# W2 by language in order of first appearance, W1 by id for twenty batches

## The chip, the core and the metric

The kernel runs on one core of a Trainium2 chip. The time is that of the device, in microseconds, as the median of timed runs; the profile is of one execution, taken apart from them. Engines are named as in the profile: PE (TensorE, with PEld for its weight loads), DVE (VectorE), ACT (ScalarE), POOL (GpSimd) and SP (SyncE, which here only issues DMAs).

## The reference

There are 128 batches of 128 rows by 512 columns in float32. Every batch has a language id, and ten languages have their own W1 (512 x 128), b1, W2 (128 x 512), b2, gamma and beta.

```python
def _L0_cond_ref(hidden_states, language_ids, W1, b1, W2, b2, gamma, beta):
    w1 = W1[language_ids]
    w2 = W2[language_ids]
    h = jnp.einsum('bsh,bha->bsa', hidden_states, w1) + b1[language_ids][:, None, :]
    h = jax.nn.relu(h)
    adapted = jnp.einsum('bsa,bah->bsh', h, w2) + b2[language_ids][:, None, :]
    x = hidden_states + adapted
    mean = jnp.mean(x, axis=-1, keepdims=True)
    var = jnp.mean(jnp.square(x - mean), axis=-1, keepdims=True)
    normed = (x - mean) * jax.lax.rsqrt(var + LN_EPS)
    return normed * gamma[language_ids][:, None, :] + beta[language_ids][:, None, :]
x = x + _L0_cond_ref(x, itok_B_0_8, L0_cond_W1, ...)
```

The ids are drawn from 0 to 8, so language 9 doesn't occur in this input, but the kernel doesn't know that. The kernel folds the outer sum in: the output is the normed row times gamma, plus (x + beta).

## The kernel before

A batch is one tile of 128 x 512. The main loop is a software pipeline with one turn per batch: in turn `i` it transposes x of batch `i` on PE, multiplies batch `i - 1` by its W1 (`down`), batch `i - 2` by its W2 (`up`), and does the residual, the statistics and the output of batch `b = i - 3` and of older ones. A helper, `keep`, pins every instruction behind the one recorded before it on its engine, so the order in the code is the order on each engine. SP issues nearly all the loads and the stores, in that same order; it takes them in turn on eight semaphores, so that a load is issued only when the load eight places before it has landed.

Per batch, PE makes four transposes of x into PSUM (`transpose_x`), four matmuls with W1 (`down`) and one with W2 (`up`); in fp32 these are issued as 4, 8 and 2 pieces. ACT copies the transposed x to SBUF (`copy_xT`), applies relu with b1 (`relu`), copies the batch's W1 out of the table of all ten languages (`stage_w1`), and squares (`square`); for every pair of batches it computes the mean and the inverse root (`scalar_means`, `deviation`). DVE adds the residual with a running sum (`residual`), subtracts the mean and multiplies by gamma (`scale`), and multiplies by the inverse deviation and adds what POOL prepared (`finish`). POOL adds beta to x (`add_beta`), and for most batches b2 to x (`add_b2`); where it doesn't, DVE adds b2 (`vector_b2`) or PE puts it into PSUM with a one-hot matmul (`pick`, inside `up`).

Tables that depend on the language are read at an offset held in a register: `lid(b, engine)` loads four ids at a time from `lang`. Since the offset isn't known when the program is built, an instruction that reads a table in this way waits for every write to the table that stands before it in the code. The transposed x has one PSUM buffer (`p_x`, bufs=1), so `transpose_x` of the next batch waits for `copy_xT` of this one.

Before the loop can run, three things are made ready.

- The rows of beta, gamma and b2 (ten each) are spread over all 128 partitions. They are split into three bf16 parts that add up to the fp32 value; a one-hot matmul on PE (`spread`, L202 to L211) picks a row into PSUM, and DVE or ACT copies it into `beta_b`, `gamma_b`, `b2_b`: 30 rows.
- W2 is loaded whole, in two loads (`load_w2`, 768 and 1792 KB).
- W1 for the first nine batches (`FIRST`) is loaded by id, 256 KB each, into a ring of five buffers; batches up to 20 (`EARLY` = 21) are copied by ACT from `w1e`, all ten W1 in a layout that loads quickly (two loads of 1280 KB); batches from 21 on are copied from `w1`, loaded in four chunks of 640 KB in the turns 8, 10, 12 and 14 (`load_w1`, L103).

PE first runs ten idle matmuls (`spin`) on a constant.

```python
if i in (8, 10, 12, 14):
    load_w1((i - 8) // 2)
...
if i + 1 >= LATE and on(i + 1):
    stage_w1(i + 1)
```

Of the kernel before, what the change touches and what calls it, by code (L numbers as in the profile page):

```python
# [16 lines left out]
P = 128  # L17
G = 4
EPS = 1e-5
FIRST = 9  # L20
EARLY = 21
LATE = 12
# [4 lines left out]
def cond_resid_kernel(ctx: ExitStack, tc: tile.TileContext, x, itok, W1, b1, W2, b2, gamma, beta, out):  # L27
# [31 lines left out]
    wp = ctx.enter_context(tc.tile_pool(name="wp", bufs=5))  # L59
# [18 lines left out]
    ids = const.tile([1, B], I32, name="ids")  # L78
# [3 lines left out]
    w1e = const.tile([P, L, KC, A], FP, name="w1e")  # L82
    w2 = const.tile([P, L * H], FP, name="w2")
    x_0 = xp.tile([P, G, H], FP, tag="x", name="x_0")
    xs[0] = x_0
# [5 lines left out]
    keep(nc.sync.dma_start(out=ids, in_=itok.rearrange("(o b) -> o b", o=1)))  # L91
    keep(nc.scalar.dma_start(out=rows[0:L, :], in_=beta))
    keep(nc.sync.dma_start(out=rows[L : 2 * L, :], in_=gamma))
    keep(nc.scalar.dma_start(out=rows[2 * L : 3 * L, :], in_=b2))
    load_part(0, 2)
    keep(nc.scalar.dma_start(out=b1r, in_=b1))

    warm = const.tile([P, 1], FP, name="warm")
    keep(nc.vector.memset(warm, 1.0))
    keep(nc.scalar.activation(warm, warm, AF.Abs_reciprocal_sqrt))  # L100
    def load_w1(k):
        keep(
            nc.sync.dma_start(out=w1[:, :, k, :], in_=W1[:, k * P : (k + 1) * P, :].rearrange("l p a -> p l a"))  # L103
        )

    ident = const.tile([P, P], FP, name="ident")
    make_identity(nc, ident)
    eps = const.tile([P, 1], FP, name="eps")
    nc.gpsimd.memset(eps, EPS)
    ones = const.tile([P, P], BF, name="ones")  # L110
    nc.gpsimd.memset(ones, 1.0)
# [3 lines left out]
    R = 3 * L  # L115
# [6 lines left out]
    keep(nc.vector.tensor_scalar(pick[:, L : 2 * L], pick[:, L : 2 * L], -0.5, None, ALU.mult))  # L122
# [4 lines left out]
    wrap = const.tile([1, B], I32, name="wrap")  # L127
    keep(nc.vector.tensor_scalar(wrap, ids, 0, L, ALU.is_lt, ALU.mult))
    lang = const.tile([1, B], I32, name="lang")
    keep(nc.vector.tensor_tensor(lang, ids, wrap, ALU.add))  # L130
    keep(nc.vector.tensor_scalar(lang, lang, 0, L - 1, ALU.max, ALU.min))

    def lid(b, engine):
        g = b // G
        if (g, engine) not in lids:
            loads, vals = nc.values_load_multi_w_load_instructions(  # L136
                lang[0:1, g * G : (g + 1) * G],
                engines=[engine],
                min_val=0,
                max_val=L - 1,  # L140
                skip_runtime_bounds_check_because="clamped on the chip to 0..L-1 above",
            )
            for ins in loads:
                keep(ins)
            lids[g, engine] = vals
        return lids[g, engine][b % G]

# [3 lines left out]
    def load_first(b):  # L151
        w1s[b] = wp.tile([P, KC, A], FP, tag="w1s", name=f"w1s_{b}")
        src = W1[bass.ds(lid(b, ET.SP), 1)].rearrange("o (p k) a -> p (o k a)", k=KC)
        keep(nc.sync.dma_start(out=w1s[b].rearrange("p k a -> p (k a)"), in_=src))

    def load_w2(lo, hi):
        dst = w2[:, lo * H : hi * H].rearrange("p (l h) -> p l h", l=hi - lo)
        keep(nc.sync.dma_start(out=dst, in_=W2[lo:hi].rearrange("l a h -> a l h")))

    def load_early(lo, hi):  # L160
        dst = w1e[:, lo:hi].rearrange("p l k a -> p l (k a)")
        keep(nc.sync.dma_start(out=dst, in_=W1[lo:hi].rearrange("l (p k) a -> p l (k a)", k=KC)))

    load_w2(0, 3)
    load_first(0)
    load_first(1)
    load_part(2, G)
    load_first(2)
    load_first(3)
    load_w2(3, L)  # L170
    xs[1] = xp.tile([P, G, H], FP, tag="x", name="x_1")
    for b in (G, G + 2):
        load_part(b, b + 2)
        load_first(b)
        load_first(b + 1)
    xs[2] = xp.tile([P, G, H], FP, tag="x", name="x_2")
    load_part(2 * G, 2 * G + 2)
    load_early(0, 5)
    load_first(2 * G)
    load_early(5, L)  # L180
    load_part(2 * G + 2, 3 * G)

    left = rp.tile([P, H], FP, tag="r", name="left")
    keep(nc.vector.tensor_copy(parts[0:R, :], rows[0:R, :]))
    keep(nc.vector.tensor_tensor(left[32 : 32 + R, :], rows[0:R, :], parts[0:R, :], ALU.subtract))
    keep(nc.vector.tensor_copy(parts[32 : 32 + R, :], left[32 : 32 + R, :]))
    keep(nc.vector.tensor_tensor(left[64 : 64 + R, :], left[32 : 32 + R, :], parts[32 : 32 + R, :], ALU.subtract))
    keep(nc.vector.tensor_copy(parts[64 : 64 + R, :], left[64 : 64 + R, :]))
# [7 lines left out]


    beta_b = const.tile([P, L * H], FP, name="beta_b")
    gamma_b = const.tile([P, L * H], FP, name="gamma_b")
    b2_b = const.tile([P, L * H], FP, name="b2_b")  # L200

    def spread(r, copier):  # L202
        t = (beta_b, gamma_b, b2_b)[r // L]
        row = p_y.tile([P, H], FP, tag="y", name=f"row_{r}")
        pick_r = pick[:, r : r + 1].to_broadcast([96, P])
        keep(nc.tensor.matmul(row, lhsT=pick_r, rhs=parts[:96, :], start=True, stop=True))
        dst = t[:, r % L * H : (r % L + 1) * H]
        if copier is nc.scalar:
            keep(nc.scalar.copy(dst, row))
        else:  # L210
            keep(nc.vector.tensor_copy(dst, row))  # L211
# [5 lines left out]
    def b2_by_matmul(b):  # L217
        return b in (5, B - 1)

    def b2_by_vector(b):  # L220
        return b < 4 or 8 <= b < B - 8 and (b % 4 == 1 if b < 24 else b % 16 in (1, 6, 11) or b % 32 == 30)

    def stage_w1(b):
        w1s[b] = wp.tile([P, KC, A], FP, tag="w1s", name=f"w1s_{b}")
        src = (w1e if b < EARLY else w1).rearrange("p l k a -> p (l k a)")[:, bass.ds(lid(b, ET.Activation) * (KC * A), KC * A)]
        keep(nc.scalar.copy(w1s[b].rearrange("p k a -> p (k a)"), src))  # L226

    def transpose_x(b):
        pxs[b] = p_x.tile([P, KC, P], FP, tag="xT", name=f"pxT_{b}")
        for k in range(KC):  # L230
            if b < EARLY:
                cols = xb(b).rearrange("s (p k) -> s k p", k=KC)[:, k, :]
            else:
                cols = xb(b)[:, k * P : (k + 1) * P]
            keep(nc.tensor.transpose(pxs[b][:, k, :], cols, ident))  # L235
# [32 lines left out]
    def up(b):  # L268
        v = lid(b, ET.PE)
        ys[b] = p_y.tile([P, H], FP, tag="y", name=f"py_{b}")  # L270
        m = b2_by_matmul(b)
        if m:
            pick_b = pick[:, bass.ds(v + 2 * L, 1)].to_broadcast([96, P])
            keep(nc.tensor.matmul(ys[b], lhsT=pick_b, rhs=parts[:96, :], start=True, stop=False))
        keep(nc.tensor.matmul(ys[b], lhsT=hT[b], rhs=w2[:, bass.ds(v * H, H)], start=not m, stop=True))  # L275
        del hT[b]
# [61 lines left out]
    def of_pair(g):  # L338
        if g not in parts_of:
            parts_of[g] = p_s.tile([P, 2], FP, tag="s", name=f"root_{g}"), st.tile([P, 2], FP, tag="part", name=f"part_{g}")  # L340
        return parts_of[g]
# [138 lines left out]
    def spin(n, width):  # L480
        idle = p_s.tile([P, H], FP, tag="s", name="idle")
# [8 lines left out]
    spin(9, H)  # L490
    spin(1, H // 2)

    def spread_turn(lo, hi):
        for r in range(lo, hi):
            spread(r, nc.scalar if r % 7 in (1, 3, 5) else nc.vector)
# [4 lines left out]

    x_turn(0)
    transpose_b1()
    spread_turn(0, 4)
    x_turn(1)
    spread_turn(4, 11)
    down(0)
    relu(0)
    spread_turn(11, 15)
    down(1)
    relu(1)  # L510
    x_turn(2)
    spread_turn(15, 19)
    x_turn(3)
    down(2)
    relu(2)
    spread_turn(19, 24)
    down(3)
    relu(3)
    spread_turn(24, R)
    up(0)  # L520
    up(1)

    for i in range(3, B + U):
# [3 lines left out]
        if i == 5:  # L527
            load_x(3)
        if i in (8, 10, 12, 14):
            load_w1((i - 8) // 2)  # L530
        if i == 4:
            up(2)
        if i == 5:
            up(3)
        if i > 3 and on(i):
            transpose_x(i)
        if b <= E:
            add_b2(b + 2)
            add_beta(b)
        if i > 4 and on(i - 1):  # L540
            down(i - 1)
        if i > 3 and on(i):
            copy_xT(i)
# [3 lines left out]
        if i > 4 and on(i - 1):  # L547
            relu(i - 1)
        if i + 1 >= LATE and on(i + 1):
            stage_w1(i + 1)  # L550
        if i > 5 and on(i - U):
# [41 lines left out]
        if FIRST <= i + 1 < LATE:  # L593
            stage_w1(i + 1)

        for n, engine in ((i + 3, ET.Activation), (i - U + 3, ET.PE), (b + 1, ET.DVE), (b + 5, ET.Pool)):
            if on(n):
                lid(n, engine)

# [36 lines left out]
```

## Time and profile before

| What | Value |
|---|---|
| Median of three runs | 308.69 us (307.93 to 308.85) |
| Span of the profiled execution | 306.5 us |
| Busy: PE, DVE, ACT, POOL | 294.6, 295.9, 282.3, 283.9 us |
| Moved by DMA | 77.85 MB, mean 254 GB/s |
| First transposes, first residual | 5.4 us, 20.9 us |

The profiled execution is known by its span; the timed runs include 2.2 us more around it. A line of the profile gives engine, line of the source, operation, the tiles by name (output on the left of the arrow, inputs on the right) and shapes. In a timeline the two numbers in front are the start and the duration in microseconds, and a bracket at the end says how long the engine was idle before and what ended that. In a table of stretches each row has the stretch, its length, the busy time of PE, PEld, DVE, ACT and POOL with the number of instructions, then the granted PE clock as a share of full speed, the DMA engines' busy share, and GB/s. `q` behind an engine's name is its sequencer, which issues DMAs and register loads. Names of DRAM tensors end in `_dram`; digits are left out of names, so `w` stands for `w1` as well as `w2`, and `b_b` for `b2_b`.

### The profile page before, as it was taken

Reading aid. Unit: us, or ns where it says so; the run is one execution under the profiler, and the core shown is the slowest. Engines: PE = TensorE matmul, PEld = TensorE weight load, DVE = VectorE, ACT = ScalarE, POOL = GpSimd, SP = SyncE. Lnnn points to the kernel's source line nnn. Section 1 sums busy time; section 2 is a strip of 40 time slices with the busy share of each in tenths; the row PEclk is TensorE's granted clock in tenths of the full one; section 3 lists DMA queues with packets and bytes.
Section 4 is the critical chain, followed back from the end, with each engine's and each line's share of the span. In section 5 each row is a group of like instructions: output and inputs, shape, how many; then the busy total and the mean of one; then the engine's idle time right before and its main releaser. Section 6 shows DMA issues by size and latency. Waiting matters only on the chain. (4 is left out here: it accounts for less than half of the span.)

```text
span 306.5 us, 6981 instructions
## 1 busy us (share of the span) xinstructions
PE 294.6 (96%) x1835; PEld 220.0 (72%) x1835; DVE 295.9 (97%) x771; ACT 282.3 (92%) x777; POOL 283.9 (93%) x238
## 2 busy tenths in 40 slices
PE   8999999999999999999999999999999999999960
PEld 3748787777777777777777777777777777777730
DVE  6889999999999999999999999999999999999985
ACT  3858999999999999999999999999999999999981
POOL 1349899999999999999999999999999999999994
PEclk9999999999999999999999999999999999999995
DMA  6999999976678766766777666767776666773324
GB/s 231 379 390 388 373 371 354 387 231 240 221 255 276 250 202 241 226 257 219 259 276 243 213 209 238 265 224 260 275 238 206 226 231 242 246 266 137 135 109 171
DMA packets 43769, 77.85 MB, mean 254 GB/s; under 512 B 1961, under 2 KB 7348, under 8 KB 43730
## 3 DMA queue, kind: packets, MB, share of 16 engines
q1 hardware_dynamic: 43382, 76.84, 72.1%
q10 hardware_dynamic: 348, 0.57, 0.5%
q8 instruction: 15, 0.25, 0.3%
q14 instruction: 24, 0.20, 0.2%
HBM read 43.85 MB, written 33.55 MB: 253 GB/s over the span
## 5 line engine op out<-in xcount | busy, mean ns | idle before, releaser
L252 POOL TENSOR_TENSOR o<-x,beta_b 128x512 f32<-128x512 f32 x128 | 173.9, 1395 | 10.2 <-DVE beta_b L211 9.5
L245 POOL TENSOR_TENSOR r<-x,b_b 128x512 f32<-128x512 f32 x97 | 135.7, 1399 | 7.3 <-DVE b_b L211 6.2
L258 PE MATMUL ph<-xT,w1s 128*128 128x128 f32 x1024 | 135.4, 275 | 0.0
L275 PE MATMUL py<-w,hT 128*128 x256 | 131.2, 595 | 0.5 <-DVE b_b L211 0.5
L258 PEld LDWEIGHTS ph<-xT,w1s 128*128 128x128 f32 x1024 | 124.9, 192 | 1.0 <-ACT hT L266 0.5
L235 PEld LDWEIGHTS pxT<-ident,x 128*128 128x128 f32 x512 | 66.6, 151 | 65.3 <-issue 49.2
L358 DVE SCALAR_TENSOR_TENSOR py<-py,nmean,gamma_b 128x512 f32<-128x512 f32 x126 | 95.0, 754 | 0.9 <-ACT sq L399 0.8
L367 DVE SCALAR_TENSOR_TENSOR o<-py,rstd,o 128x512 f32<-128x512 f32 x122 | 91.2, 748 | 0.0
L315 ACT ACTIVATE sq<-py,sum 128x512 f32<-128x512 f32 x124 | 85.9, 693 | 2.8 <-DVE py L292 2.5
L235 PE MATMUL pxT<-ident,x 128*128 128x128 f32 x512 | 78.2, 276 | 0.0
L239 ACT COPY xT<-pxT 128x512 f32<-128x512 f32 x128 | 74.7, 584 | 3.5 <-PE pxT L235 3.5
L292 DVE SCALAR_TENSOR_TENSOR py<-py,r 128x512 f32<-128x512 f32 x97 | 67.0, 691 | 0.2
L226 ACT COPY w1s<-w 128x512 f32 x107 | 65.5, 612 | 0.0
L266 ACT ACTIVATE hT<-ph,b1T 128x128 f32<-128x128 f32 x128 | 46.9, 366 | 7.9 <-PE ph L258 2.6
L275 PEld LDWEIGHTS py<-w,hT 128*128 128x128 f32 x256 | 39.1, 192 | 2.9 <-issue 1.0
L315 ACT ACTIVATION_READ_ACCUMULATOR sq<-py,sum 128x1 f32 x124 | 25.0, 202 | 0.0
L292 DVE SCALAR_TENSOR_TENSOR py<-py,x 128x512 f32<-128x512 f32 x31 | 21.7, 699 | 0.4
L285 DVE TENSOR_TENSOR py<-py,b_b 128x512 f32<-128x512 f32 x29 | 20.2, 695 | 0.7 <-PE py L275 0.6
L325 ACT ACTIVATE root<-ssq,eps 128x2 f32<-128x2 f32 x62 | 16.4, 265 | 0.0
L292 DVE DVE_READ_ACCUMULATOR py<-py,r 128x1 f32 x97 | 13.7, 141 | 0.0
L306 ACT ACTIVATE nmean<-sum 128x2 f32<-128x2 f32 x62 | 12.3, 198 | 0.0
L329 DVE SCALAR_TENSOR_TENSOR part<-ssq,root 128x2 f32<-128x2 f32 x62 | 9.3, 151 | 0.2 <-ACT root L325 0.2
(55 smaller groups left out, 90.4 us busy)
## 6 DMA issues: line engine op xcount, KB each, us to landing
out_dram<-o SPq DMA_DIRECT2D x61, 512.0 KB, 3.4
x<-in_x_dram SPq DMA_DIRECT2D x29, 1024.0 KB, 6.2
x<-in_x_dram SPq DMA_DIRECT2D x6, 512.0 KB, 8.8
w1e<-in_L_cond_W_dram SPq DMA_DIRECT2D x2, 1280.0 KB, 12.3
w<-in_L_cond_W_dram SPq DMA_DIRECT2D x4, 640.0 KB, 8.1
w1s<-in_L_cond_W_dram SPq DMA_DIRECT2D x9, 256.0 KB, 8.4
w<-in_L_cond_W_dram SPq DMA_DIRECT2D x1, 1792.0 KB, 10.3
w<-in_L_cond_W_dram SPq DMA_DIRECT2D x1, 768.0 KB, 5.4
```

The costliest lines, as they stand in the source:

```text
L226: keep(nc.scalar.copy(w1s[b].rearrange("p k a -> p (k a)"), src))
L235: keep(nc.tensor.transpose(pxs[b][:, k, :], cols, ident))
L239: keep(nc.scalar.copy(xT[b], pxs.pop(b)))
L245: keep(nc.gpsimd.tensor_tensor(rs[b], xb(b), b2_b[:, bass.ds(v * H, H)], ALU.add))
L252: keep(nc.gpsimd.tensor_tensor(os[g][:, j, :], xb(b), beta_b[:, bass.ds(v * H, H)], ALU.add))
L258: nc.tensor.matmul(phs[b], lhsT=w1s[b][:, k, :], rhs=xT[b][:, k, :], start=(k == 0), stop=(k == KC - 1))
L266: keep(nc.scalar.activation(hT[b], phs.pop(b), AF.Relu, bias=b1T[:, bass.ds(lid(b, ET.Activation), 1)]))
L275: keep(nc.tensor.matmul(ys[b], lhsT=hT[b], rhs=w2[:, bass.ds(v * H, H)], start=not m, stop=True))
L292: nc.vector.scalar_tensor_tensor(ys[b], ys[b], 1.0, r, ALU.mult, ALU.add, accum_out=col(sums, b))
L315: nc.scalar.activation(sq, ys[b], AF.Square, bias=col(sums, b), scale=-float(H), accum_out=col(ssqs, b))
L358: nc.vector.scalar_tensor_tensor(ys[b], ys[b], col(nmeans, b), gamma_b[:, bass.ds(v * H, H)], ALU.add, ALU.mult)
L367: nc.vector.scalar_tensor_tensor(o, ys.pop(b), rstds[g][:, j : j + 1], o, ALU.mult, ALU.add)
```

## The change

**W1.** The first 20 batches (`BY_ID`) take W1 by id, 256 KB each, into a ring that now has seven buffers; `w1e` and its two loads are gone. From batch 20 on, ACT copies W1 from `w1` as before. The loads for batch `n` are issued by `ahead(n)`, five turns ahead in the loop; `ahead` also loads x in pairs, W2, and at `n` = 9, 12, 15 and 18 the four chunks of `w1`. In the loop, `load_w1` is called with the same chunk numbers again in the turns 16, 21, 26 and 31, where it was called in the turns 8 to 14 before.

**W2.** It is no longer loaded whole. The kernel ranks the languages by first appearance among the ids: every language, on its own partition, takes the largest weight (a falling function of the position) among the batches that have it; a matmul puts these on one row for comparison, a count of larger ones is its rank, and two small matmuls turn ranks into `slots`, a list that has the language of each slot and the slot of each batch. SP loads W2 for slot after slot (ten loads of 256 KB, `load_slot`), and `up` reads it at the batch's slot. Since batch `b` has a slot of at most `b`, `up(b)` of the first ten batches waits only for the slots up to `b`.

**Rows.** Beta's ten rows are loaded four times, once for every 32 partitions, and spread by DVE with `stream_shuffle` from SBUF to SBUF. Gamma's and b2's rows still go through one-hot matmuls; gamma's are copied by ACT ahead of the loop, b2's by DVE and ACT in turn during turns 3 to 7. The first eight batches (`BY_PE`) get b2 by the matmul inside `up`, where it was DVE for batches 0 to 3, POOL for 4, 6 and 7, and the matmul for 5. The bf16 parts are made by reading the upper halves of the fp32 words.

**Order.** POOL adds beta two batches earlier than before. In a turn, `copy_xT` stands before `down`. The idle matmuls are seven instead of ten.

```diff
-FIRST = 9
-EARLY = 21
-LATE = 12
+BY_ID = 20
+BY_PE = 8
+RING = 7
...
+    keep(nc.sync.dma_start(out=lang[:, 0:B], in_=itok.rearrange("(o b) -> o b", o=1).to_broadcast([L, B])))
+    keep(nc.scalar.dma_start(out=rows[0:L, :], in_=gamma))
+    load_part(0, 1)
+    keep(nc.scalar.dma_start(out=rows[L : 2 * L, :], in_=b2))
+    for q in range(4):
+        engine = nc.sync if q % 2 else nc.scalar
+        keep(engine.dma_start(out=beta_rows[32 * q : 32 * q + L, :], in_=beta))
+    keep(nc.scalar.dma_start(out=b1r, in_=b1))
+    load_part(1, 2)
...
+    keep(nc.vector.scalar_tensor_tensor(seen, lang, own, weight, ALU.is_equal, ALU.mult))
+    keep(nc.vector.tensor_reduce(first, seen, mybir.AxisListType.X, ALU.max))
...
+    def rank_languages():
+        order = p_s.tile([P, H], FP, tag="s", name="order")
+        keep(nc.tensor.matmul(order[:L, 0:L], lhsT=first.to_broadcast([L, L]), rhs=ident[:L, :L], start=True, stop=True))
...
+        keep(nc.vector.tensor_scalar(above, order[:L, 0:L], first, None, ALU.is_gt, ALU.add, accum_out=rank))
+        keep(nc.vector.tensor_scalar(own_of, lang[:, 0:B], own, None, ALU.is_equal))
+        keep(nc.vector.tensor_scalar(place, count[:, 0:L], rank, None, ALU.is_equal))
...
+    def place_languages(order):
+        keep(nc.tensor.matmul(order[:1, L : 2 * L], lhsT=own, rhs=place, start=True, stop=True))
+        keep(nc.tensor.matmul(order[:1, 2 * L : 2 * L + B], lhsT=rank, rhs=own_of, start=True, stop=True))
+        keep(nc.vector.tensor_copy(slots, order[:1, L : 2 * L + B]))
...
+    def load_slot(j):
+        if j == 0:
+            v = lid(0, ET.SP)
+        else:
+            if not perm:
+                perm.extend(values(slots[0:1, 1:L], ET.SP, L - 1))
+            v = perm[j - 1]
+        src = W2[bass.ds(v, 1)].rearrange("o a h -> a (o h)")
+        keep(nc.sync.dma_start(out=w2[:, j * H : (j + 1) * H], in_=src))
...
+    def spread_beta(lo, hi):
+        for r in range(lo, hi):
+            keep(nc.vector.stream_shuffle(beta_b[:, r * H : (r + 1) * H], beta_rows, [r] * 32))
...
-        return b in (5, B - 1)
+        return b < BY_PE or b == B - 1
...
-        src = (w1e if b < EARLY else w1).rearrange("p l k a -> p (l k a)")[:, bass.ds(lid(b, ET.Activation) * (KC * A), KC * A)]
+        src = w1.rearrange("p l k a -> p (l k a)")[:, bass.ds(lid(b, ET.Activation) * (KC * A), KC * A)]
...
+    def ahead(n):
+        if n in (4, 6, 8, 10):
+            load_part(n, n + 2)
+        load_by_id(n)
+        if n < L + 2:
+            load_slot(n - 2)
+        if n >= 9 and n % 3 == 0:
+            load_w1((n - 9) // 3)
...
-        if i in (8, 10, 12, 14):
-            load_w1((i - 8) // 2)
...
+        if i in (16, 21, 26, 31):
+            load_w1((i - 16) // 5)
+        b2_rows = [r for r in (2 * i - 6, 2 * i - 5) if 0 <= r < L]
...
+        if i + RING - 2 < BY_ID:
+            ahead(i + RING - 2)
...
-        if i + 1 >= LATE and on(i + 1):
+        if BY_ID <= i + 1 and on(i + 1):
             stage_w1(i + 1)
```

## The prediction

> **What bounds the kernel now.** I read the page's busy times first, then stretches of ten microseconds (busy time by engine, granted clock, DMA share, GB/s), then the instructions of two turns of the loop in order of time, then the DMA issues, the waits, and last the clock at the end of the run.
>
> ```profile
> PE 294.6 (96%) x1835; PEld 220.0 (72%) x1835; DVE 295.9 (97%) x771; ACT 282.3 (92%) x777; POOL 283.9 (93%) x238
> 0.00:10.00 10.00, 8.76 (x35) 4.39 (x36) 7.25 (x19) 4.85 (x9) 0.87 (x8) 1.00 0.74 270
> 10.00:20.00 10.00, 9.54 (x60) 6.57 (x59) 7.77 (x13) 7.04 (x15) 2.83 (x3) 1.00 1.02 381
> 20.00:30.00 10.00, 10.00 (x58) 7.26 (x57) 9.63 (x23) 7.41 (x21) 10.00 (x9) 1.00 1.05 388
> 30.00:40.00 10.00, 10.00 (x65) 7.91 (x65) 9.87 (x29) 9.36 (x26) 8.86 (x8) 1.00 1.07 376
> 40.00:50.00 10.00, 10.00 (x64) 7.84 (x63) 10.00 (x25) 9.72 (x27) 9.89 (x9) 1.00 1.07 354
> 50.00:60.00 10.00, 10.00 (x66) 7.82 (x66) 10.00 (x27) 9.71 (x30) 9.46 (x9) 1.00 1.06 386
> 60.00:70.00 10.00, 10.00 (x66) 7.60 (x65) 10.00 (x28) 9.83 (x28) 10.00 (x9) 1.00 0.77 264
> ```
>
> From 20 us on four engines are full at once, so a wait on any of them is not won back later. The DMA engines are full too, but only until 60 us. Summing the GB/s column, 2.7, 6.5, 10.4, 14.2, 17.7 and 21.6 MB have moved by 10, 20, ... 60 us, 377 GB/s from 10 us on.
>
> ```profile
> 55.65 0.62 ACT L226 COPY w1s<-w1e 128x512 f32 x1
> 56.01 0.63 PE L235 MATMUL pxT<-ident,x 128*128 128x128 f32 x4
> 56.16 0.70 ACT L315 ACTIVATE sq<-py,sum 128x512 f32<-128x512 f32 x1
> 56.83 0.59 ACT L239 COPY xT<-pxT 128x512 f32<-128x512 f32 x1
> 57.57 0.37 ACT L266 ACTIVATE hT<-ph,b1T 128x128 f32<-128x128 f32 x1
> 57.83 0.61 ACT L226 COPY w1s<-w 128x512 f32 x1
> 58.23 0.60 PE L235 MATMUL pxT<-ident,x 128*128 128x128 f32 x4
> 59.16 0.27 ACT L325 ACTIVATE root<-ssq,eps 128x2 f32<-128x2 f32 x1
> 59.56 0.76 DVE L358 SCALAR_TENSOR_TENSOR py<-py,nmean,gamma_b 128x512 f32<-128x512 f32 x1
> 60.09 0.61 ACT L226 COPY w1s<-w 128x512 f32 x1
> ```
>
> The turn is 2.2 us. The copies at L226 are those of W1 for batches 20, 21 and 22. Behind each stand, on ACT, the square of an older batch, the copy of the next transposed x and the relu. VectorE's scale starts 0.1 us after ACT's root, and PE's next transposes start 0.8 us after the copy of xT began: an ACT wait reaches both almost whole.
>
> ```profile
> x<-in_x_dram SPq DMA_DIRECT2D x29, 1024.0 KB, 6.2
> w<-in_L_cond_W_dram SPq DMA_DIRECT2D x4, 640.0 KB, 8.1
> 297.00:300.00 3.00, 0.00 (x0) 0.00 (x0) 2.19 (x11) 2.28 (x7) 2.92 (x3) 1.00 0.06 21
> 300.00:302.00 2.00, 0.00 (x0) 0.00 (x0) 1.96 (x7) 0.37 (x1) 1.92 (x3) 0.50 0.34 131
> 1.19 4.45 PE L484 MATMUL idle<-ones 128*128 128x512 bf16 x10 [1.19 <-POOL ones L111]
> ```
>
> A load takes microseconds to land. PE's last matmul ends at 296.3 and 3.7 us later its clock is halved; the opening matmuls took 0.43 us each, the same 512 columns later 0.22.
>
> **The sum's base.** The profiled execution spans 306.5 us; the median of the three timed runs, 308.69, is 2.2 above. I add the parts to 306.5 and carry the 2.2.
>
> **Head, up to batch 10: -3.0, which the next part swallows.** PE's path: first x lands near 3.5 (512 KB took 3.6 from issue, 256 KB stores 2.0), W1 of batch 0 near 6.2, then two downs (0.89 each), seven gamma rows (0.22), one up with its pick (1.08): batch 3's transposes start near 11.1. Three gamma rows follow (0.66), five turns of 2.84 (transposes 0.43, two b2 rows 0.44, down 0.89, pick 0.22, up 0.86) and two of 2.40: batch 10 at 30.8, where it was 33.8. VectorE: ten shuffles have no row; the row copies of L211 took 3.82 for 6, so 0.64, and GpSimd's pass over the same tile, 1.24, is the far bound (nothing moves 512 columns in under the 0.58 of ACT's copy). I take 0.64, the same engine and tile: 6 to 12.4 us (18.5 at the far bound), before the first residual is due at about 13 (20.9 today). VectorE also loses 12 row copies against ten shuffles and four b2 adds (0.67 each); GpSimd loses three adds (1.24 each) and starts near 13 instead of 11, ACT loses eleven copies of W1 (0.51 each) and does 15 row copies instead of 13, and two of the splits. The ranking adds some eight small VectorE instructions (0.15 to 0.28 each, as at L122 to L131) and three small matmuls; the slots are there near 6.3, and SP, which needs them for its second W2 load with every later load behind it, gets there near 7. The 8 loads already issued (5.6 us of moving) cover it if it is late. The four beta loads (20 KB, two of them on SP ahead of x 1) cost SP 0.7, which is in the lag below. I cost all of it at nothing: the wait for the loads hides it, up to some 8 us; without that cover the head is worth the 3.0.
>
> **DMA order: +8.0 at batch 22.** All loads stand in SP's one queue, each behind the one eight places before. In units of 256 KB, what must have landed for batch 20's copy of w1 is x to 23 (24), W1 by id (20), W2 (10), four chunks of w1 (10), five stores (10) and the first chunk again (2.5): 76.5 units, 20.1 MB. The chunks are loaded twice: `ahead` issues them at batches 9, 12, 15, 18, and the loop again at i = 16, 21, 26, 31; the second loads are 2.6 MB more. The copies read w1 at a register's offset, so each waits for all chunks issued before it, and each reload after the first waits for the copy before. On today's curve 20.1 MB is reached at 56.4. Add 0.7, because only 0.5 MB instead of 1.3 is issued before the ids are known (bounds 0 and 1.5), and 1.4 from moving to landing (x of batches 24 to 27 is issued at 49.7, lands 8.4 later, and ends 20.3 MB in order, which the curve reaches at 56.8): 58.5. ACT stands there from 52.7 (55.65 - 3.0). It copies batch 21's W1 at about 60.5, and that releases the second reload, which is queued behind x 24 to 31 and two stores: 91 units, 23.9 MB with small ones, on the curve at 66.4, landed at 68.5. Batch 22's copy then starts at 68.5 instead of 60.1: +8.4, less 0.3 that VectorE and PE have in hand. SP's issues (0.36 to 0.47 each) are shorter than the 0.70 that 256 KB take to move, so the queue does not run dry.
>
> **The other two reloads: +3.6 and +2.2.** The queue is empty by then (share 0.77 and less). For batch 27: the copy of batch 26 ends at 69.4 on today's clock, but SP first waits for the store of batches 18 and 19 (finished at 69.8, issue 0.4). 640 KB land after 4.1 (3.6 for 512 KB in the quiet head; bounds 3.6, and 5.7, the fastest 1 MB load) plus 0.5 for that store: 74.9 against a copy due at 71.0, less 0.3. For batch 32 no store stands between: 80.3 + 0.1 + 4.1 = 84.5 against 82.0, less 0.3.
>
> **Clock: +1.3.** PE runs out of work for about 5.7 us before batch 23's transposes, longer than the 3.7 us after which the clock fell. The opening spin shows half speed for at most the first 5.3 us of work (2.6 us lost); below it is 0. I take the middle. The first wait's share is hidden by the second, the last two are shorter than 3.7. [...]
>
> Sum: 306.5 + 8.0 + 3.6 + 2.2 + 1.3 = 321.6, with 2.2 around it 323.8. After batch 32 the turn is 2.19 as before, and the tail is the same code.
>
> **Rivals.** (1) The DMA keeps ahead: batch 20's copy finds everything landed, and only three round trips are paid: -3.0, then 4.2 - 1.7 (the turn less one copy) - 0.3 = 2.2, 3.6, 2.2: 313.7. For it: waits for a landing were 1.1 and 0.5 us today. Against: a share over 1.0 up to 60 us, and more bytes. 10%. (2) Faster: the second loads hold nobody up, because nobody waits for them; then the head's gain counts, less 1.5 for W1 of batch 19 (72 units, 55.3, due 53.5): about 307. It decides at the landing: a reload that took under 1.7 us would do the same, and the shortest landing in the trace is 2.0. The copies' waits on the reloads stand in the built program. 8%. (3) Loads of 256 KB move more slowly: at three quarters of 377 GB/s the 34 of them among the 91 units (8.9 MB) take 7.9 us longer: 331.7. Against: from 10 to 20 us, with loads of 256 and 512 KB, the rate was 381, as good as any. 6%. [...]
>
> **Numbers.** Forecast 74%: its own range is 318 to 332 (a rate of 390 or 354 GB/s after 10 us puts batch 22 at 66.6 or 72.2; the bounds of landing give 1.8 to 5.2 and 1.7 to 3.8 at the reloads; 0 to 2.6 for the clock). 2% is left for what I don't see. The range, 312 to 330, adds the first rival, leaves the second and third out, and cuts the corner where every bound is at its worst. Measured runs differ by 0.3%, so faster means under 307.8: 9%, same 2%, slower 89%.
>
> **What would show it.** The ACT copies of w1 for batches 20, 22, 27 and 32 wait for a DMA, by about 6, 6, 4 and 2.5 us, and no other does; the DMA share stays over 1.0 to about 66 us; PE's clock dips once near 69 us; four more 640 KB loads are listed. Wrong would be: no waits at these copies, or batch 22's at 61 (first rival); rows of beta later than 19 us; a slower turn after batch 32.

## The result, and the profile after

The changed kernel takes 330.3 us (median, 329.2 to 331.8) beside 308.6 for the kernel before on the same chip: a ratio of 1.071, with a 95% interval from 1.068 to 1.074. It is slower, as forecast, but by 21.7 us instead of 15.1, and 0.3 us beyond the upper end of the range. The profiled execution spans 328.8 us, 22.3 more than before.

Busy times, and of the picture in 40 slices the rows for the PE clock and for the DMA, of the changed kernel:

```profile
PE 301.3 (92%) x1835; PEld 223.3 (68%) x1835; DVE 296.9 (90%) x780; ACT 280.3 (85%) x770; POOL 281.2 (86%) x239
...
PEclk9899999988989899999999999999999999999995
DMA  5999999955478267777765757686667777762344
```

Every engine has about as much to do as before, and the span is longer: the time went into waits. A slice is 8.2 us; the clock is reduced in the second and around 72, 90 and 107 us. The stretches of ten microseconds show where the waits lie (columns as before: PE, PEld, DVE, ACT, POOL busy, clock, DMA share, GB/s):

```profile
10.00:20.00 10.00, 9.81 (x56) 6.80 (x55) 5.72 (x15) 8.86 (x21) 6.85 (x6) 0.96 1.01 351
...
30.00:40.00 10.00, 9.08 (x54) 6.34 (x53) 10.00 (x22) 6.62 (x20) 5.96 (x5) 1.00 1.07 394
...
50.00:60.00 10.00, 9.54 (x59) 7.08 (x59) 9.83 (x28) 7.33 (x21) 8.01 (x7) 1.00 1.09 379
60.00:70.00 10.00, 7.15 (x44) 4.97 (x42) 8.11 (x21) 4.42 (x13) 10.00 (x9) 1.00 0.99 338
70.00:80.00 10.00, 7.18 (x41) 6.13 (x42) 4.83 (x13) 8.10 (x23) 6.57 (x6) 0.83 0.37 115
80.00:90.00 10.00, 6.09 (x36) 4.22 (x35) 5.67 (x18) 5.53 (x16) 8.62 (x7) 0.97 0.56 181
...
100.00:110.00 10.00, 6.83 (x36) 4.86 (x34) 6.50 (x18) 5.86 (x16) 7.57 (x7) 0.83 0.72 244
```

In the last four rows PE is busy for 6 to 7 us of ten, VectorE and ACT are not full either, and the DMA share falls to 0.37: everything waits for single loads. The instructions of ACT in order of time name them; the copies at L285 are those of W1 for batches 20, 21, 22, 27 and 32:

```profile
60.02 0.61 ACT L285 COPY w1s<-w 128x512 f32 x1
62.21 0.61 ACT L285 COPY w1s<-w 128x512 f32 x1
71.00 0.62 ACT L285 COPY w1s<-w 128x512 f32 x1 [6.42 <-DMA w<-in_L_cond_W_dram]
87.11 0.62 ACT L285 COPY w1s<-w 128x512 f32 x1 [4.39 <-DMA w<-in_L_cond_W_dram]
103.44 0.62 ACT L285 COPY w1s<-w 128x512 f32 x1 [3.91 <-DMA w<-in_L_cond_W_dram]
```

The loads that they wait for stand in SP's order of time, and in the list of DMA issues there are eight of 640 KB where there were four:

```profile
51.85 0.53 SPq L114 DMA_DIRECT2D w<-in_L_cond_W_dram  x1
62.84 0.70 SPq L114 DMA_DIRECT2D w<-in_L_cond_W_dram  x1
81.96 0.42 SPq L114 DMA_DIRECT2D w<-in_L_cond_W_dram  x1
97.79 0.38 SPq L114 DMA_DIRECT2D w<-in_L_cond_W_dram  x1
...
w<-in_L_cond_W_dram SPq DMA_DIRECT2D x8, 640.0 KB, 7.7
```

The second, third and fourth reload (the second loads of the chunks) let the copy start 8.2, 5.1 and 5.6 us after their issue. Batch 20's copy waits for no load: the first reload, issued at 51.85, had landed 7.7 us later, at 59.6, and ACT reached the copy at 60.0. How much later PE begins the transposes of a batch than in the kernel before tells what each of these costs:

| Batch | 10 | 20 | 22 | 23 | 24 | 27 | 29 | 32 | 35 | 127 |
|---|---|---|---|---|---|---|---|---|---|---|
| Later by, us | 3.2 | 4.4 | 4.4 | 10.2 | 11.6 | 11.6 | 17.4 | 17.4 | 22.5 | 22.5 |

So there are two parts: 4.4 us up to batch 20 (called the head below; the forecast had a gain of 3.0 by batch 10), and 7.2, 5.8 and 5.1 us at the three reloads.

### The profile page after: what moved, and what is told of

It is laid out like the page before. It is cut to its first block, busy times and chain, and to the rows that moved or that the text cites. A ratio compares the mean times of both kernels' runs of the same rounds, so it can differ in the third digit from the quotient of the medians.

```text
span 328.8 us, 7103 instructions
## 1 busy us (share of the span) xinstructions
PE 301.3 (92%) x1835; PEld 223.3 (68%) x1835; DVE 296.9 (90%) x780; ACT 280.3 (85%) x770; POOL 281.2 (86%) x239
## 5 line engine op out<-in xcount | busy, mean ns | idle before, releaser
L311 POOL TENSOR_TENSOR o<-x,beta_b 128x512 f32<-128x512 f32 x128 | 163.7, 1294 | 29.8 <-DMA out_dram<-o 13.8
L317 PE MATMUL ph<-xT,w1s 128*128 128x128 f32 x1024 | 138.4, 279 | 0.8 <-DMA w1s<-in_L_cond_W_dram 0.8
L334 PE MATMUL py<-w,hT 128*128 (+1 forms) x256 | 132.9, 601 | 0.0
L304 POOL TENSOR_TENSOR r<-x,b_b 128x512 f32<-128x512 f32 x94 | 121.8, 1297 | 12.4 <-DMA w<-in_L_cond_W_dram 7.4
L317 PEld LDWEIGHTS ph<-xT,w1s 128*128 128x128 f32 x1024 | 128.0, 196 | 1.8 <-issue 1.1
L294 PE MATMUL pxT<-ident,x 128*128 128x128 f32 x512 | 79.6, 279 | 13.3 <-ACT xT L298 12.7
L285 ACT COPY w1s<-w 128x512 f32 x108 | 66.2, 613 | 14.7 <-DMA w<-in_L_cond_W_dram 14.7
L351 DVE SCALAR_TENSOR_TENSOR py<-py,r 128x512 f32<-128x512 f32 x94 | 64.8, 689 | 2.9 <-PE py L334 2.6
L351 DVE SCALAR_TENSOR_TENSOR py<-py,x 128x512 f32<-128x512 f32 x34 | 23.7, 697 | 0.3
L344 DVE TENSOR_TENSOR py<-py,b_b 128x512 f32<-128x512 f32 x25 | 17.3, 690 | 0.9 <-PE py L334 0.8
L351 DVE DVE_READ_ACCUMULATOR py<-py,r 128x1 f32 x94 | 13.1, 139 | 0.0
L388 DVE SCALAR_TENSOR_TENSOR part<-ssq,root 128x2 f32<-128x2 f32 x62 | 10.9, 175 | 0.2 <-ACT root L384 0.2
```

The source lines that it names most:

```text
L304: keep(nc.gpsimd.tensor_tensor(rs[b], xb(b), b2_b[:, bass.ds(v * H, H)], ALU.add))
L311: keep(nc.gpsimd.tensor_tensor(os[g][:, j, :], xb(b), beta_b[:, bass.ds(v * H, H)], ALU.add))
L317: nc.tensor.matmul(phs[b], lhsT=w1s[b][:, k, :], rhs=xT[b][:, k, :], start=(k == 0), stop=(k == KC - 1))
L351: nc.vector.scalar_tensor_tensor(ys[b], ys[b], 1.0, r, ALU.mult, ALU.add, accum_out=col(sums, b))
```

## The experiments

The theory was that the second loads of the chunks cost by the waits of the copies (theory A), not by their bytes (theory B). Four runs, each with or without one thing:

```diff
# e1: the changed kernel, chunks loaded once
-        if i in (16, 21, 26, 31):
-            load_w1((i - 16) // 5)
# e2: the kernel before, with these two lines added
# e3: the second loads go into a tile of their own, that nobody reads
-            load_w1((i - 16) // 5)
+            k = (i - 16) // 5
+            keep(nc.sync.dma_start(out=spare, in_=W1[:, k * P : (k + 1) * P, :].rearrange("l p a -> p l a")))
# e4: the second loads bring one language of ten, 64 KB
+            keep(nc.sync.dma_start(out=w1[:, 0:1, k, :], in_=W1[0:1, k * P : (k + 1) * P, :].rearrange("l p a -> p l a")))
```

> The changed kernel with the four chunks of w1 loaded once: the second loads in the turns 16, 21, 26 and 31 are left out. Theory A (the copy of W1 for batches 22, 27 and 32 waits for the reload before it, and each wait costs its length and a stretch of half clock): the shifts measured at the three waits, 7.2, 5.8 and 5.1 us, go, so 330.3 - 18.1 = 312.2; no ACT wait for a load at the copies, no half clock between 70 and 110 us. Theory B (the extra 2.6 MB fill the DMA queues, waits are only where this shows): also near 312, since the bytes go too; the third run tells the two apart. Theory C (the loop itself is slower, whatever the reloads): 325 or more. In A and B batch 20's transposes stay near 60.4, 4.4 later than in the kernel before.

> The kernel before with second loads of the four chunks of w1 added in the turns 16, 21, 26 and 31, and nothing else changed. Theory A: three waits of 4 to 6.5 us at the copies of batches 22, 27 and 32 and three stretches of half clock, 15 to 18 us in all: 324 to 327. Theory B: 2.6 MB more at 377 GB/s is 7 us at most: 309 to 316.

> The changed kernel with the second loads going to a spare tile that nothing reads: the same bytes in the same turns, and no copy waits for them. Theory A: as with the chunks loaded once, 311 to 314. Theory B: most of the loss stays, 319 or more.

> The changed kernel with the second loads cut to one language, 64 KB instead of 640, into the same tile, so the copies wait as before. Theory A: the round trip stays, the moving of 576 KB (1.5 us) goes and whatever the many pieces cost: a landing near 2.5 us from the issue, waits of about 1 to 1.5 us at batches 22, 27 and 32, too short for the clock to fall: 312.2 + 3 to 4 = 315 to 316. Theory B: a tenth of the bytes, 312 to 313.

| Kernel | Time, us | Ratio to before (95%) |
|---|---|---|
| e1: chunks once | 314.1 | 1.020 (1.017 to 1.023) |
| e2: before, chunks twice | 325.5 | 1.055 (1.050 to 1.059) |
| e3: same bytes, nobody waits | 312.7 | 1.013 (1.011 to 1.015) |
| e4: a tenth of the bytes, copies wait | 321.8 | 1.043 (1.041 to 1.045) |

The two lines cost 16.2 us in the changed kernel (330.3 less 314.1) and 16.8 in the kernel before (325.5 less 308.7), where nothing else was changed. With the same bytes into a tile that nobody reads they cost nothing (e3, 312.7, beside 314.1). The waits are the cause; the bytes cost only by making the waits longer. With a tenth of the bytes about half of the cost is still there (321.8 less 314.1 is 7.7); in the order of time on ACT, the kernel with small reloads has for batches 22, 27 and 32

```profile
68.61 0.62 ACT L285 COPY w1s<-w 128x512 f32 x1 [3.92 <-DMA w<-in_L_cond_W_dram]
83.26 0.62 ACT L285 COPY w1s<-w 128x512 f32 x1 [1.47 <-DMA w<-in_L_cond_W_dram]
96.25 0.62 ACT L285 COPY w1s<-w 128x512 f32 x1 [2.23 <-DMA w<-in_L_cond_W_dram]
```

that is 5.6, 2.6 and 4.0 us after the issues at 62.96, 80.69 and 92.29. So of the 8.2, 5.1 and 5.6 us of the full reloads 2.5, 2.6 and 1.7 come with their size. I had expected 315 to 316 here.

**The clock after a wait.** Each wait cost PE more than its own length (7.2, 5.8 and 5.1 us for waits of 6.42, 4.39 and 3.91). This run gives PE idle matmuls at the end of turns 22 and 32:

```diff
+        if i in (22, 32):
+            spin_small({22: 20, 32: 11}[i])
```

> The changed kernel with idle matmuls on PE at the end of turns 22 (twenty) and 32 (eleven), so that PE has work during the first and the third wait for a reload. Theory (each wait costs the wait and then 0.8 to 1.4 us more, because the clock is halved for 3.4 us after it): the clock stays full after batches 22 and 32 and the time falls by about 2.2 us, from 330.3 to 328. Rival (the extra is lag of the pipeline behind the wait and would be there at full clock): no change, 330 to 331. The second wait, at batch 27, is left as it is and keeps its halved clock in both.

The time was 329.3 us (327.4 to 331.3, two runs), 1 us lower than the changed kernel's and within the scatter of both, so it decides nothing. The trace, of the run of 331.3 us, says more. First the clock row of the changed kernel with idle matmuls, then its ACT copies:

```profile
PEclk9999999999959999999999999999999999999995
```

```profile
73.29 0.62 ACT L285 COPY w1s<-w 128x512 f32 x1 [6.28 <-DMA w<-in_L_cond_W_dram]
89.72 0.62 ACT L285 COPY w1s<-w 128x512 f32 x1 [5.94 <-DMA w<-in_L_cond_W_dram]
106.01 0.62 ACT L285 COPY w1s<-w 128x512 f32 x1 [2.85 <-DMA w<-in_L_cond_W_dram]
```

The clock stays full at the first and third wait, and PE's lag grows by 5.8 and 2.4 us there: the wait less 0.5. At the second, without idle matmuls, it is halved for 6.8 us, and the lag grows by 8.4, which is the wait plus 2.5. Only the first wait, of 6.28 us, shows what the idle matmuls do: third waits of 2.93 us in e2 and 2.80 in g4 (below) left the clock full without them, with the lag growing by 2.5 and 2.4 there. In the changed kernel the clock is halved for 3.41 us at each of the three waits (from 72.3, 89.4 and 106.4 us on), and by the rule of the wait less 0.5 that costs 1.3, 1.9 and 1.6 us. The profiled run gained nothing: its head was 2.4 us longer (batch 20 was 6.8 us late), and its second wait 1.6 us longer.

All runs together show at which waits it fell. Behind the head PE stood idle for 3.06 us or more twelve times (three in the changed kernel, three in f3, two each in e2 and g4, one each in e4 and e5), and each time the clock was halved; after idle stretches of 2.19 us or less it never was. Nothing between the two was met.

**The head.** Without second loads, 5.4 us are left (314.1 less 308.7), all of them lost by batch 20, whose transposes come 5.6 us late here (4.4 in the changed kernel, from which 312.2 was expected). The lag of PE's transposes grows there in steps of 0.7 and 1.1 us at batches 12 and 16, and the order of time on PE names two reasons:

```profile
42.60 0.72 PE L294 MATMUL pxT<-ident,x 128*128 128x128 f32 x4 [0.49 <-ACT sq L374]
...
52.64 0.72 PE L294 MATMUL pxT<-ident,x 128*128 128x128 f32 x4 [0.90 <-DMA x<-in_x_dram]
```

Yet what batch 12's transposes need of ACT, the copy that frees their PSUM buffer, had ended at 41.0 us, and the x of batch 16, issued at 34.6, had landed at 42.6. What did end last (at 42.4 and 52.4) was a register load on PE's own sequencer: those of `slots`, at 40.13 us for 2.26 and at 50.04 for 2.40. The line of the register loads in the kernel with chunks once (duration in ns as least, median and most):

```profile
L185 PEldq TENSOR_LOAD <-slots x39: 298/999/2396, 16.3 to 288.8; - x39
...
L185 PEldq TENSOR_LOAD <-lang x3: 343/346/527, 11.1 to 299.7; - x3
```

Of the 39 loads of `slots` the first nine bring one word each, in 0.30 to 0.32 us; the other 30 bring four words, as those of `lang` do, and took 1.0 us or more. Those of `lang` begin at a multiple of 16 bytes in their tile; those of `slots` begin 8 bytes past one, since the list starts 40 bytes in, behind the ten languages. Seven runs follow this up. Each of f1, f2, g1, g2 and g3 adds to the one before, starting from chunks once; f3 is the changed kernel with the edits of f1 and f2, and g4 with all five.

```diff
# f1: batches' slots begin 12 words in, not 10 (PAD = 12 for L wherever slots is written or read)
-            lids["slots", g] = values(slots[0:1, L + g * G : L + (g + 1) * G], ET.PE, L - 1)
+            lids["slots", g] = values(slots[0:1, PAD + g * G : PAD + (g + 1) * G], ET.PE, L - 1)
# f2: also register loads ahead, and more idle matmuls
-    spin(6, H)
+    spin(7, H)
-    spin(1, H // 2)
+    spin(1, H)
...
     x_turn(1)
+    spin(2, H)
...
     spread_gamma(0, 4)
+    lid(0, ET.PE)
+    slot(0)
     x_turn(2)
+    slot(1)
...
     down(1)
+    slot(2)
...
     up(0)
+    slot(3)
...
+        if i == 5:
+            lid(4, ET.PE)
# g1: also
-    op = ctx.enter_context(tc.tile_pool(name="op", bufs=5))
+    op = ctx.enter_context(tc.tile_pool(name="op", bufs=6))
# g2: also
-            pool, tag = (st, "root") if 2 * g < BY_PE else (p_s, "s")
+            pool, tag = (st, "root") if g < 2 else (p_s, "s")
# g3: also
-                perm.extend(values(slots[0:1, 1:L], ET.SP, L - 1))
-            v = perm[j - 1]
+                perm.extend(values(slots[0:1, 0:L], ET.SP, L - 1))
+            v = perm[j]
```

> The changed kernel with the chunks of w1 loaded once (314.1 us before), and the list of slots padded from 10 to 12 words ahead of the batches' slots, so that each register load of four slots starts at a multiple of 16 bytes, as those of four ids do. In the kernel with chunks once PE's register loads of four slots took 1.0 to 2.4 us each, those of four ids 0.33. Theory (a load of four words that are not aligned is slow, and the two of 2.26 and 2.40 us at 40.1 and 50.0 us held up the transposes of batches 12 and 16 by 0.7 and 1.2 us): they take about 0.3 us, the steps at batches 12 and 16 are gone, and the time falls by about 2 us, to 312. Rival 1 (PE there waits for the x of batch 16, as the waits list it): the steps stay, 314. Rival 2 (loads of the register are slow because of the tile or the traffic, not the address): they stay at 1 us or more, 314.

> The kernel with chunks once and aligned slots, and two more changes in the head: the register loads of the first batches' slots on PE are made one to two turns ahead instead of between the pick's weights and its matmul (0.4 us in each of three turns), and there are three and a half more idle matmuls ahead of the first down, so that the clock is full from 4 us on (it was half until 12.3 us). Theory (PE bounds the head: its work of 3.45 us a turn in turns 3 to 6 and the half clock are what costs): batch 10's transposes start 3 to 3.5 us earlier than with chunks once, at about 34, and the time is near 309. Rival (loads or VectorE bound the head): batch 10 is early but batch 20 is where it was, and the time is that of aligned slots alone, about 312.

> The kernel with chunks once and the head mended (312.6 us before), with six output tiles instead of five. There GpSimd waited 6.55 us, from 32.3 to 38.9, for the store of the first pair to land before it could write the sixth pair's tile, and 4.25 us for the rows of b2, and its last additions stand 4.4 us later than in the kernel before, PE's last transposes only 1.8. Theory (GpSimd is behind from the head and sets the end): the long wait moves one pair on and shrinks to about 1.5 us, GpSimd's last additions stand less than 1 us behind, and the time falls by about 2 us, to 310.7. Rival (PE or VectorE set the end): the wait goes and the time stays at 312.6.

> The same with the inverse roots of pairs 2 and 3 in PSUM instead of SBUF, as those of later pairs are. With the roots in SBUF VectorE's small instructions on 128x2 that read them took up to 1.24 us beside an addition on GpSimd, and 0.15 without. Theory (two operands in SBUF slow them beside GpSimd, and this is on the path: PE's step of 1.3 us at batch 14 follows the slow ones of pair 3 at 39.0 and 40.7): those of pairs 2 and 3 take 0.15, the step at batch 14 is gone, and the time falls by 1.0 to 1.5 us against six output tiles alone, to 309.5. Rival (their length is a wait that the record includes): they stay long, and the time stays.

> The same with SP's list of languages by slot loaded into registers from its start, ten words at a multiple of 16 bytes, instead of nine from the second word on: that load took SP 1.9 us, with every later load queued behind it. Theory: it takes about 0.6 us, the second W2 load is issued 1.3 us earlier, and since the loads of the first batches are not what batches 2 to 10 wait for, the time stays within 0.5 us of the run before. Rival (the DMA engines' 281 GB/s from 5 to 10 us cost the head): 1 us faster.

| Kernel | Time, us | Ratio to before (95%) | Span | Batch 20's transposes later by | POOL's addition of beta for batch 126 later by |
|---|---|---|---|---|---|
| e1: chunks once | 314.1 | 1.020 (1.017 to 1.023) | 312.1 | 5.6 | 5.2 |
| f1: slots aligned | 313.2 | 1.016 (1.014 to 1.018) | 311.2 | 3.4 | 5.6 |
| f2: loads ahead, idle matmuls | 312.6 | 1.014 (1.012 to 1.015) | 310.2 | 1.1 | 4.4 |
| g1: six output tiles | 313.8 | 1.014 (1.010 to 1.017) | 312.2 | 6.1 | 3.5 |
| g2: roots in PSUM | 309.5 | 1.003 (1.002 to 1.004) | 307.4 | 0.2 | 1.2 |
| g3: SP's list aligned | 309.1 | 1.002 (1.001 to 1.003) | 306.9 | 0.4 | 0.5 |

With the slots aligned the same line reads

```profile
L186 PEldq TENSOR_LOAD <-slots x39: 299/330/1047, 15.6 to 286.3; - x39
```

and the steps at batches 12 and 16 are gone. That is the theory, against both rivals: neither x nor ACT was what PE waited for there. Not all of PE's 2.2 us by batch 20 is due to this: 1.0 us was there by batch 10, with the clock full from 10.9 us on instead of 12.3, and a new step of 0.8 us at batch 14 takes back part of the two. Of the 2.2 us, moreover, 0.9 reached the end, and of the next 2.4 (f2, whose two changes were not tried apart, and which was expected near 309) only 0.6. The last two columns show why: POOL is as full as the others in the loop (in the kernel before 9.46 to 10.00 us of ten from 40 to 70 us), and it was still 4 to 6 us behind. In the order of time on POOL, of the kernel f2:

```profile
27.34 1.28 POOL L305 TENSOR_TENSOR r<-x,b_b 128x512 f32<-128x512 f32 x1 [4.25 <-ACT b_b L269]
...
38.86 1.27 POOL L312 TENSOR_TENSOR o<-x,beta_b 128x512 f32<-128x512 f32 x1 [6.55 <-DMA out_dram<-o]
```

POOL adds beta two batches earlier than before, so it needs the sixth pair's output tile when the first pair's store has not landed. A sixth tile (g1) ends that wait: the longest wait for a store is then 1.8 us. The time, however, did not fall to 310.7; at 313.8 it is not better than f2. VectorE's part of the order of time shows what came instead. In g1 the small instructions on 128x2 that read the roots are

```profile
35.82 1.19 DVE L389 SCALAR_TENSOR_TENSOR part<-ssq,root 128x2 f32<-128x2 f32 x1
37.59 0.64 DVE L391 SCALAR_TENSOR_TENSOR part<-part,root 128x2 f32<-128x2 f32 x1
38.76 0.69 DVE L394 SCALAR_TENSOR_TENSOR rstd<-part,root 128x2 f32<-128x2 f32 x1
```

and in g2, with the roots of these pairs in PSUM,

```profile
34.01 0.14 DVE L389 SCALAR_TENSOR_TENSOR part<-ssq,root 128x2 f32<-128x2 f32 x1
34.73 0.14 DVE L391 SCALAR_TENSOR_TENSOR part<-part,root 128x2 f32<-128x2 f32 x1
35.40 0.15 DVE L394 SCALAR_TENSOR_TENSOR rstd<-part,root 128x2 f32<-128x2 f32 x1
```

With its sixth tile POOL worked on from 32 to 39 us, and these instructions met its additions, which take 1.27 us each. In g1 eight of the twelve for the first four pairs took 0.6 to 1.24 us, 6.3 us more than 0.15 each; in f2 the excess was 3.9, and the three of pair 2, which ran while POOL stood still (33.6 to 35.0 us), took 0.15 each with both operands in SBUF. VectorE is full at that time (10.00 of 10.00 from 30 to 40 us), so this is on the path. Over f2, g1's tile and g2's roots together are worth 3.1 us; the tile alone was worth nothing. The runs don't tell whether the roots in PSUM alone would do: that combination wasn't run. g1 has a second thing against it, the clock: in its profiled execution it was full only from 10.4 us, in f2's from 5.4, and batch 3 was 2.2 us later for that. From batch 3 to batch 14 PE then lost 5.2 us in g1 and 2.5 in f2, which is no matter of the clock; in g2, where it was full from 5.8 us, 1.2.

In the kernel before, where the roots of all pairs are in PSUM, the first of the three (L329 there) took 0.146 to 0.157 us in all 62 pairs, with POOL busy for 93% of the span. So the slow ones had both operands in SBUF and an addition of 1.27 us on POOL beside them, and took up to 1.24 us; with one operand in PSUM it was 0.14 in g2. What in the two engines makes them slow no run shows.

Aligning SP's list (g3) shortened its register load from 1.88 to 0.97 us. The time was 0.4 us lower, with intervals that overlap, as its theory had it. So the 5.4 us of the head are traced to register loads on PE, the clock of the head, POOL's wait for an output tile, and POOL and VectorE in each other's way; what remains is 0.4 us, about what can be measured. No version here beats the kernel before.

**Head and reloads together.** The forecast costed the head at nothing because the wait for the loads would hide it. Two runs put the mended head under the second loads:

> The changed kernel (chunks loaded twice) with the same three mends as in the run before: aligned slots, register loads ahead, idle matmuls in the head. The prediction costed the head at nothing because the wait for the loads would hide it. If that holds here, batch 20's copy of W1 now waits for the first reload, which lands at about 59.5, by some 3 us, and the time stays within 1.5 us of the changed kernel's 330.3. If the head's delay counts in full, the time falls by as much as the mends save without the second loads, 4 to 5 us, to 325.5.

> The changed kernel (chunks loaded twice) with all five mends of the head. With three of them batch 20's copy of W1 waited 1.6 us for the first reload, which landed near 60.4 us, and that copy stood only 0.5 us later than in the changed kernel although its head was 1.3 us shorter. Theory (the loads hide the head, as the prediction had it, and what the reloads cost beyond it is fixed): batch 20's copy waits 3 to 5 us and starts near 60 us, the copies for batches 22, 27 and 32 wait for about 5, 4.4 and 3.9 us, and the time is 325.5 to 327.5, that is 16 to 18 us above the same mends without the second loads. Rival (head and reloads add up): 309.5 plus the 16.2 between the changed kernel and chunks once, with batch 20's copy not waiting.

They took 327.6 us (two runs, 328.9 and 326.4; ratio 1.062, 1.057 to 1.067) and 326.2 (1.055, 1.049 to 1.060). The first lies between the two times expected for it and doesn't decide between them. The copies for batches 20, 22, 27 and 32 in g4:

```profile
60.04 0.62 ACT L286 COPY w1s<-w 128x512 f32 x1 [1.95 <-DMA w<-in_L_cond_W_dram]
69.66 0.62 ACT L286 COPY w1s<-w 128x512 f32 x1 [5.31 <-DMA w<-in_L_cond_W_dram]
86.11 0.62 ACT L286 COPY w1s<-w 128x512 f32 x1 [4.43 <-DMA w<-in_L_cond_W_dram]
101.34 0.62 ACT L286 COPY w1s<-w 128x512 f32 x1 [2.80 <-DMA w<-in_L_cond_W_dram]
```

Batch 20's copy stands at 60.02 us in the changed kernel, at 60.48 in f3 and at 60.04 here, though PE reached batch 20's transposes 1.3 us (f3) and 2.0 us (g4) earlier. It waits 1.6 and 2.0 us for the first reload instead. So up to this copy the wait does hide the head, as forecast; the wait was shorter than expected because the head of g4 was 2.4 us late at batch 20, not 0.4 as in g3, with five mends the same: the clock was full from 10.4 us on, in g3 from 4.1, and by batch 3 that had made a difference of 2.0. What the second loads cost over the mended head is 17.2 us (326.2 less 309.1), beside 16.2 over the head as it was. The time still fell by 4.1 us, and PE's transposes show where. By batch 24 they gained 1.1: batch 22's copy started 7.0 us after the issue of its reload instead of 8.2. At the last reload they gained 2.7: the wait was 1.1 us shorter, and PE's idle time of 2.06 us, instead of 3.17, left the clock full. Why these two waits were shorter the runs don't show.

## Why the prediction was right or wrong

| Step | Predicted, us | Measured in the profile after, us |
|---|---|---|
| Head up to batch 10 | -3.0, hidden | +3.2 at batch 10, +4.4 at batch 20; hidden but for 0.5 (copy at 60.0, reload landed at 59.6) |
| Batch 22's copy, without clock | +8.0 | +10.3 (4.4 from the head and 6.42 - 0.5 from the wait) |
| Reload for batch 27 | +3.6 | +3.9 (4.39 - 0.5) |
| Reload for batch 32 | +2.2 | +3.4 (3.91 - 0.5) |
| Clock | +1.3, once | +1.3, +1.9 and +1.6 |
| Sum over the base of 306.5 | 15.1 | 22.4; the span is 22.3 longer |

**Right.** The mechanism, as e1 to e3 show: a copy at a register's offset waits for all reloads ahead of it, and each reload waits for a copy. The places were right for batches 22, 27 and 32, not for batch 20, whose copy was to wait for about 6 us and did not wait. The four further 640 KB loads are listed, the DMA share is 1.01 or more from 10 to 60 us (0.99 from 60 to 70), the ten shuffles stand 0.63 us apart and were done at 13.1 us, and the slots were there at 6.5. After batch 35 nothing more is lost.

**The clock, 3.5 us too small, failed most.** It was priced once, since "the last two are shorter than 3.7" us. PE stood idle for 5.67, 3.91 and 3.17 us at the three reloads, and the clock fell at each; the last is shorter than 3.7, as are 3.18 in e4 and 3.06 in f3, where it fell too. The 3.7 was one reading, at the end of the kernel before. In the fourteen kernels profiled here the clock fell 1.7 to 5.0 us after the last matmul, and in the changed kernel the three falls lie 17.07 us apart, five times the 3.41 that each halved stretch lasted; so the one distance from the last matmul, 3.7, did not tell at which wait it would fall. The size of one loss was within the bounds given (0 to 2.6); the number of losses was wrong. The halved stretches at the waits are 3.41 or 6.83 us, and in the head the clock was full from 12.3 us in e1, from 10.9 in f1, and, with the same idle matmuls, from 5.4 in f2, 10.4 in g1 and 4.1 in g3. By half of 3.41, 1.7 a wait, three waits would come to 5.1; measured are 4.8.

**Batch 22, 2.3 us too small.** The copy was forecast at 68.5 us and came at 71.0. The copy of batch 21, which releases the second reload, was put at 60.5 and stood at 62.2. The first reload, put at 58.5, landed at 59.6 (60.3 in f3, 59.9 in g4), and ACT reached batch 20's copy 0.5 us after that. The rest, 0.8, is the copy's own 0.6 us and the issue behind it at 62.84. From the release on, 8.2 us to the start of the copy are close to the 8.0 forecast.

**The other reloads, 0.3 and 1.2 too small.** They took 5.1 and 5.6 us from issue to the copy, against 4.1 taken and bounds of 3.6 and 5.7. The nearest rows were the right ones, and the value lies at their upper end.

**The head, a sign wrong but little of it paid.** Batch 10's transposes came at 37.0 us, not at 30.8. Half of this was there at batch 3, at 14.1 instead of 11.1: W1 of batch 0, put near 6.2, landed at 7.5, and the clock, taken as full, was halved from 7.45 to 10.86 us (half of 3.41 is 1.7). The other half is in the turns. Three of the five of 2.84 us took 3.3 to 3.45, with two register loads on PE's queue in each, one of them between the pick's weights and its matmul; the two of 2.40 took 2.9 and 3.4, and in them PE waited 0.27 and 0.52 us for VectorE. SP came to its second W2 load at 9.7, not "near 7": nine registers took 1.88 us. Register loads were in no step of the forecast, although every one of them stands in its engine's queue. With the reloads the cover held up to batch 20's copy, so this cost the sum about 0.5 there; without them it would have cost the forecast 8.4, from -3.0 to +5.4 (e1).

**The rivals.** The first, that batch 20's copy finds everything landed, came true at that copy, though by a later ACT (60.0 us instead of 52.7) and not by an earlier load, and its time, 313.7, did not. The second is what e3 built: when nobody waits, the second loads cost nothing (312.7 beside 314.1); the time is then 312.7 and not 307, because of the head. The third, slower moving of 256 KB loads, has no support: from 20 to 60 us 379 to 394 GB/s were moved, and no run shows the three quarters of 377 that it took.

## What to carry to other kernels

A load that overwrote a table in use made the next reader whose address is in a register wait for its whole way from release to landing (3.9 to 6.4 us of waiting for 640 KB in the changed kernel), even when it brought few bytes (64 KB still cost 1.5 to 3.9); look for the release in the queue order, not at the bandwidth, and load once. Where PE stood still for 3.06 us or more, its clock was halved each time, so add the clock to each such wait, not once: 1.3 to 1.9 us in the changed kernel. And count register loads as instructions of their engine's queue: begin lists of several words at multiples of 16 bytes (four words on PE took 0.33 us instead of 1.0), and load them turns ahead (f2, tried only together with idle matmuls: 0.6 us).

## What the runs showed of the hardware that I had not expected

- On PE a register load of four words took 0.33 us from an address at a multiple of 16 bytes in its tile (f1; once 1.05, at 39 us) and 1.0 us from one 8 bytes past it (e1; up to 2.4, at 40 and 50 us). One word took 0.30 to 0.34 us, wherever in the list it stood. On SP ten words from such a multiple took 0.97 us, and nine from the second word on 1.88. The engine matters too: four words of the aligned `lang` took VectorE 0.61 us (median, e1).
- A wait that the trace puts down to a DMA or to ACT (0.49 and 0.90 us at batches 12 and 16 in e1) was such a register load, of 2.26 and 2.40 us; aligning the list removed the wait (f1).
- VectorE's 128x2 instructions with both operands in SBUF took up to 1.24 us beside an addition on GpSimd, 0.15 while GpSimd stood still (f2), and 0.14 with one operand in PSUM (g2). With a sixth output tile, with which GpSimd worked on, eight of twelve took 0.6 us or more (g1), with five tiles five of twelve (f2).
- A reload of 64 KB took 2.6 to 5.6 us from issue to the start of the copy that waits for it (e4), a reload of 640 KB 5.1 to 8.2 in the changed kernel and 4.5 to 9.6 over all kernels with such waits.
- The clock of PE was halved at each of twelve idle stretches of 3.06 us or more and at none of 2.19 or less. In the changed kernel the third halving began at 106.4 us, 1.2 us after PE had work again (105.3).
